# Count and selection behind the first experts, and output products over two blocks, in a convolution, attention and experts kernel

## The chip, the cores and the metric

The kernel runs on one core of a Trainium2 chip. The metric is the device time of one execution in microseconds (us). Everything is computed in 32-bit floating point.

## The reference

The input `x` has the shape (4, 128, 64, 64): four images, 128 channels, 4096 positions each. Two layers follow each other. The first is a convolutional attention: group normalisation, three 1x1 convolutions with PReLU, a softmax over 4096 x 4096 scores for each image, and the result added to `x`. The second works on the 4096 positions as tokens of 128 numbers: a layer normalisation and a causal attention with eight heads and cumulative sums, added to the tokens; then the part that this change is about:

```
logits = einsum('bsd,ed->bse', x, gate_w) + gate_b        # 64 experts
probs = softmax(logits, axis=1)                           # over the 4096 tokens
vals, idx = top_k(probs.transpose(0, 2, 1), 8)            # 8 tokens for each expert
pooled = the 8 gathered tokens, weighted by vals          # one row per image and expert
h = gelu([pooled, 1] @ weight1)                           # 128 -> 512
out = [h, 1] @ weight2                                    # 512 -> 128
outputs.at[idx].add(out * vals)                           # back to the 8 tokens
```

The experts' output is added to the tokens and turned back to channels by positions.

## The kernel before

**Layout.** The tile `t` holds 128 chunks of 128 tokens, that is 32 blocks of 512 tokens, eight for each image. The gate's logits of image `b` are kept in `lg[b]` as 128 partitions (two halves of a block times 64 experts) by 8 x 256 numbers. The first 2,200 us are the attention of layer 0 and the loop over the 32 blocks of layer 1. While the loop runs, the gate's logits, the eight greatest of each block, the candidates' rows (gathered by GpSimd from a table in DRAM) and, for images 0 to 2, the count, the selection and the pooling are spread over it by a plan (`make_plan`, slots named by block and place).

**Order.** TensorE (PE) has the order of the program everywhere. VectorE (DVE), ScalarE (ACT) and GpSimd (POOL) have it for `loop()` and `last_choice()`; for `experts()` and `stores()` the framework's scheduler places their instructions. Each engine works through its own queue in order. SyncE (SP) issues nearly all DMAs, in order too.

**The end of the kernel** is what the change touches.

- `last_choice()` (from L1434) finishes image 3, whose last block is complete only when the loop ends. ACT takes the root of the variances (`gate_root`, L1236), DVE the reciprocals (`gate_close`, L1243), ACT and DVE together normalise (`gate_norm`), PE turns (`gate_turn`, L1275) and multiplies (`gate_logits`, L1282), DVE adds the bias and takes the eight greatest (L1290). They are merged with those of the seven earlier blocks; a product with `swap` (`pw`, L1453) brings the other half's. ACT takes the exponentials (`ce`, `chd`, and L1473 for the whole of `lg`), DVE spreads the candidates' weights (`dd`, L1379), and PE pools the gathered tokens (`pp`, L1486, L1493, L1497). A product gives the sums of the exponentials (`pq`, L1502), their reciprocal is spread over partitions (`dr`, L1505; `pr`, L1510), and `pooled` is written (L1515).
- `fill` (L1419) and `put_back` (L1431) turn blocks of `t` to channels by positions in the meantime: PE transposes four chunks to PSUM, and a copy writes them back. Ten blocks are turned here, the other 22 by `turn_back` (L1583, L1584) under the experts.
- `count` (L1350) counts how many logits reach the eighth greatest, in two pieces of 1,024 columns; `select` (L1358) sets the others to zero in 2,048 columns. For image 3 `late_choice()` calls both. The count serves only a check (`late_count`, `row_check`); the selection is needed by the last stage.
- `experts()` goes over 16 groups of four experts. `first(g)` (L1620) multiplies the pooled rows by `weight1`, `turn(g)` (L1631, L1637, L1642) turns, adds the bias and applies GELU, `second(g)` (L1649) multiplies by `weight2`. An expert's weights are 512 KB. 21 experts find a place before (`load_into`, L1572); the other 43 are loaded in halves, `reload1` (L1558) and `reload2` (L1565), each into the place of an expert whose product is done. Twice `spread` (L1664, L1668) brings the experts' rows to `eo`.
- `z_at` are small selection matrices for `spread`; POOL builds them (L1593, L1595).
- `stores()` (L1703 to L1719) goes over the 32 blocks: two products (one for each half) of `eo` with the selected logits, each of 256 columns, into a PSUM tile of which there are two; DVE adds the tile to `t` (L1714), or in every fifth block ACT copies it (L1711) and POOL adds it (L1712); SP writes two blocks to DRAM at a time, at both ends one.

Of the kernel before, what the change touches and what calls it, by code (L numbers as in the profile page):

```python
# [17 lines left out]
def conv_attn_hybrid_kernel(  # L18
# [809 lines left out]
    def fast():  # L828
# [405 lines left out]
        def gate_root(m, count):  # L1234
# [4 lines left out]
            )  # L1239

        def gate_close(m, count):
            at = slice(ring(m), ring(m) + count)
            nc.vector.reciprocal(env.grs[:, at], env.grs[:, at])  # L1243
            nc.vector.scalar_tensor_tensor(  # L1244
                out=env.gnb[:, at], in0=env.gmv[:, at, :, 0:1].rearrange("p m c o -> p m (c o)"),
                scalar=-1.0, in1=env.grs[:, at], op0=ALU.mult, op1=ALU.mult,
            )
# [98 lines left out]

        def count(b):
            st = sel[b]
            for j in range(2):
                nc.vector.tensor_scalar(  # L1350
                    out=env.e2b[:, :HD], in0=flat_lg(b, CPB * j, CPB * j + CPB),
                    scalar1=st["ce"][:, 16:17], scalar2=None, op0=ALU.is_ge, op1=ALU.add,
                    accum_out=st["sums"][:, 2 + j : 3 + j],
                )
# [78 lines left out]
        def last_choice():  # L1433
# [42 lines left out]
            )  # L1476
            put_back(8, act, 2)
            cw = weigh_candidates(b)
# [16 lines left out]
            for h in range(2):  # L1495
                for j in range(2):
                    nc.tensor.matmul(  # L1497
                        pp, x2[:, 2 * h + j, :], ct[:, j, h * E : (h + 1) * E],
                        start=False, stop=(h == 1 and j == 1),
                    )  # L1500
            pq = ps.tile([P, BLK], F32, tag="t", name="f_pq3")
            nc.tensor.matmul(pq[:, 0:1], env.pair, sums[:, 0:1], start=True, stop=True)  # L1502
# [15 lines left out]

        def late_choice():
            count(B - 1)  # L1520
            select(B - 1)

# [52 lines left out]
        def slot_of(room, i):  # L1575
            return room[:, bass.ts(i, HD)]
# [9 lines left out]
        def experts():  # L1586
# [4 lines left out]
            ]  # L1591
            for b, z in enumerate(z_at):
                nc.gpsimd.memset(z, 0.0)  # L1593
                for h in range(2):
                    nc.gpsimd.tensor_copy(  # L1595
                        z[:, 32 + h * E : 64 + h * E].rearrange("p (g u) -> p g u", u=QG),
                        ident.rearrange("p (u g b) -> p b g u", u=QG, b=B)[:, b],
                    )
            fb1s = env.e1b[:, HD : HD + E * FC].rearrange("p (e c) -> p e c", c=FC)
# [7 lines left out]
            for tile_ in hold:  # L1607
                nc.gpsimd.memset(tile_, 0.0)
            hr = env.rest.tile([P, FH], F32, tag="xl", name="f_hr", bufs=3)

            def own(tile_, g):
# [85 lines left out]
        def stores():  # L1697
            for n in range(NB):
                b, k = blocks[n]
                sc = ps.tile([P, 2, BLK], F32, tag="kv", name=f"f_sct_{n}", bufs=2)  # L1700
                for h in range(2):
                    half = slice(h * E, (h + 1) * E)
                    nc.tensor.matmul(  # L1703
                        sc[:, h, :HB], env.eo[half, b, :], env.lg[b][half, k, :],
                        start=True, stop=True,
                    )
                at = bass.ds(n * CPB, CPB)
                view = t[:, at, :].rearrange("p (h c) x -> p h (c x)", h=2)
                if n % 5 == 3:
                    part = env.rest.tile([P, 2, HB], F32, tag="xl", name=f"f_scs_{n}", bufs=3)  # L1710
                    nc.scalar.copy(part, sc[:, :, :HB])  # L1711
                    nc.gpsimd.tensor_tensor(view, view, part, ALU.add)  # L1712
                else:
                    nc.vector.tensor_add(view, view, sc[:, :, :HB])  # L1714
                ends = n < 2 or n >= NB - 2
                if ends or k % 2:
                    lo = n if ends else n - 1
                    at = bass.ds(lo * CPB, (n + 1 - lo) * CPB)
                    nc.sync.dma_start(  # L1719
                        out=out[b, :, bass.ds((lo % NBLK) * BLK, (n + 1 - lo) * BLK)],  # L1720
                        in_=t[:, at, :].rearrange("p i c -> p (i c)"),
                    )
# [316 lines left out]
        def make_plan():  # L2039
# [55 lines left out]
            at(NB - 1, "T", merge_halves, B - 1)  # L2095
            at(NB - 1, "T", gathers, B - 1, 0, 8)

        def loop():
# [71 lines left out]
            assert not plan, plan.keys()  # L2170

        with tc.manual_schedule(engines={mybir.EngineType.PE}):
            layer0(env)
# [4 lines left out]
            with tc.manual_schedule(  # L2178
# [5 lines left out]
                last_choice()  # L2184
            for room in (slot_of(env.ama, 0), slot_of(env.ama, 1), slot_of(env.ama, 2),
                         slot_of(env.ama, 3), env.wvs,
                         env.held[:, bass.ts(3, HD)]):
                load_into(room)
            for i in range(CPB):
                load_into(slot_of(env.amb, i))  # L2190
            load_into(slot_of(env.e2a, 0))
            load_into(slot_of(env.e2a, 1))
            load_into(slot_of(env.e1b, 0))
            load_into(env.e1b[:, 5 * BLK : 7 * BLK])
            experts()
            stores()
        fp.close()
# [73 lines left out]
```

## Time and profile before

| what | value |
|---|---|
| median of three runs | 2334.75 us (2324.92 to 2334.96) |
| the profiled execution | 2316.78 us, span 2315.1 us |
| PE busy | 2246.9 us (97%) |
| DVE busy | 1439.6 us (62%) |
| ACT busy | 1086.3 us (47%) |
| POOL busy | 196.6 us (8%) |
| mean granted TensorE clock | 0.994 |
| DMA | 105.82 MB, mean 46 GB/s |

The span is the time from the first to the last instruction. PEld is the load of a stationary operand into TensorE, which overlaps with PE. A row of a group names the line of the program, the engine, the operation, output and inputs, shapes and count; then its busy time in us and the mean of one in ns, and the idle time of the engine just before it with what ended most of it. A timeline row begins with start and duration in us. A row of stretches gives for each engine the busy us and the number of instructions, then the clock that TensorE was granted as a share of full speed, the busy share of the DMA engines, and GB/s. A product in 32-bit numbers appears as two matmul instructions, so "x8" is four products.

### The profile page before, as it was taken

How to read it: one execution, taken by the hardware profiler on the slowest of the kernel's cores; microseconds unless marked ns; L12 is line 12 of the kernel's file. 1: busy time of each engine (PE TensorE's matmuls, PEld its weight loads, DVE VectorE, ACT ScalarE, POOL GpSimd, SP SyncE). 2: the span in 40 equal slices, each digit the busy share in tenths (PEclk: the TensorE clock that was granted, in tenths of full speed). 3: DMA queues.
4: the chain of work that ended last, by engine and by line, in shares of the span. 5: the costliest groups of instructions: out<-in, count | busy, mean ns of one | idle time of the engine just before them, and what ended most of it. 6: DMA issues, size and time to landing. Idle time of an engine off the chain costs nothing.

```text
span 2315.1 us, 43294 instructions
## 1 busy us (share of the span) xinstructions
PE 2246.9 (97%) x18418; PEld 1174.0 (51%) x18418; DVE 1439.6 (62%) x2332; ACT 1086.3 (47%) x1324; POOL 196.6 (8%) x365
## 2 busy tenths in 40 slices
PE   7999999999999999999999999999999999999987
PEld 3544444444444444444444444455655656656653
DVE  7666565655665565565556666567777777875623
ACT  2343333433333443334454544445665666665641
POOL 0000000000000000000000000012212222123401
PEclk9999999999999999999999999999999999999989
DMA  2000010000010000001000000011111121114577
GB/s 79 30 12 17 9 45 8 17 8 9 17 45 9 9 17 8 9 12 40 9 5 5 5 10 5 20 44 35 47 58 48 49 64 46 52 57 135 186 261 288
DMA packets 79067, 105.82 MB, mean 46 GB/s; under 512 B 9232, under 2 KB 45072, under 8 KB 78864
## 3 DMA queue, kind: packets, MB, share of 16 engines
q1 hardware_dynamic: 77264, 99.81, 13.7%
q8 instruction: 146, 2.39, 0.4%
q0 software_dynamic: 1024, 2.10, 0.3%
q10 hardware_dynamic: 576, 1.05, 0.1%
q14 instruction: 57, 0.47, 0.1%
HBM read 79.60 MB, written 17.04 MB: 42 GB/s over the span
## 4 chain that ended last, share of the span: by engine, by line
PE 88%; DVE 5%; ACT 3%; DMA 3%; issue 1%; SPq 0%; POOL 0%; ACTq 0%; DVEq 0%; POOLq 0%
PE av L1887 36%; PE sc L1862 18%; PE f_pv L1128 9%; PE f_pk L973 8%; PE f_pt L1151 3%; PE f_po L1174 2%; PE pd L1913 1%; PE f_po L1186 1%; PE pa L1835 1%; PE pe L1809 1%; ACT f_e1a L980 1%; DMA x<-in_x_dram 1%; PE f_pl L1282 1%; PE otr L1925 1%; PE f_ltr L965 1%
## 5 line engine op out<-in xcount | busy, mean ns | idle before, releaser
L1887 PE MATMUL av<-pr,am 64*128 64x512 f32 x4096 | 976.4, 591 | 3.0 <-ACT pr L1867 3.0
L1867 ACT ACTIVATE pr<-sc 128x1024 f32<-128x1024 f32 x512 | 523.6, 1023 | 781.3 <-PE sc L1862 768.1
L1874 DVE TENSOR_TENSOR acc<-acc,pr 128x1024 f32<-128x1024 f32 x480 | 586.5, 1222 | 484.2 <-ACT pr L1867 479.9
L1887 PEld LDWEIGHTS av<-pr,am 64*128 64x128 f32 x4096 | 401.2, 187 | 472.6 <-issue 457.1
L1862 PE MATMUL sc<-e,e 64*128 64x512 f32 x2048 | 534.5, 591 | 4.8 <-DMA e<-side 4.8
L1862 PEld LDWEIGHTS sc<-e,e 64*128 64x128 f32 x2048 | 201.4, 187 | 236.3 <-issue 228.6
L1128 PE MATMUL f_pv<-f_held,f_ama 128*32 128x256 f32 x4096 | 237.5, 381 | 5.7 <-ACT f_e1a L980 4.6
L973 PE MATMUL f_pk<-f_held,f_ama 128*128 128x512 f32 x512 | 234.9, 603 | 0.0
L1133 ACT ACTIVATE f_amb<-f_pv 128x1024 f32<-128x1024 f32 x128 | 130.7, 1023 | 125.2 <-PE f_pv L1128 125.1
L981 DVE TENSOR_TENSOR f_e1a<-f_e1a,f_held 128x1024 f32<-128x1024 f32 x128 | 156.6, 1224 | 48.7 <-ACT f_e1a L980 48.4
L980 ACT ACTIVATE f_e1a<-f_pk 128x1024 f32<-128x1024 f32 x128 | 129.9, 1025 | 119.4 <-PE f_pk L973 54.7
L1128 PEld LDWEIGHTS f_pv<-f_held,f_ama 128*32 128x32 f32 x4096 | 129.5, 110 | 99.7 <-ACT f_e1a L980 10.9
L982 DVE TENSOR_REDUCE f_e1a<-f_e1a 128x8 f32<-128x1024 f32 x128 | 155.3, 1218 | 3.5
L973 PEld LDWEIGHTS f_pk<-f_held,f_ama 128*128 128x128 f32 x512 | 92.5, 190 | 108.6 <-issue 101.0
L1092 POOL COPY f_held<-f_e1a 32x32 f32<-32x32 f32 x128 | 30.8, 240 | 892.8 <-DVE f_e1a L1074 559.1
L918 POOL MEMSET f_held<- 128x1024 f32 x1 | 1.0, 956 | 1036.0 <-DVE xn L1800 1036.0
L1151 PE MATMUL f_pt<-f_amb,f_held 128*32 128x128 f32 x1920 | 83.1, 276 | 0.8 <-ACT f_amb L1133 0.8
L1151 PEld LDWEIGHTS f_pt<-f_amb,f_held 128*32 128x32 f32 x1920 | 59.9, 109 | 10.3 <-issue 5.2
L1192 DVE TENSOR_TENSOR t<-t,f_po 128x512 f32<-128x512 f32 (+1 forms) x33 | 22.1, 671 | 56.7 <-PE f_po L1186 56.7
L956 ACT ACTIVATE f_xl<-t,ln_nb,ln_rs 128x128 f32<-128x128 f32 x128 | 52.8, 490 | 0.9 <-PE pa L1835 0.9
L1263 ACT ACTIVATE f_x<-t,f_gnb,f_grs 128x128 f32<-128x128 f32 x126 | 51.3, 482 | 0.4 <-DVE f_gnb L1244 0.4
L1871 DVE COPY acc<-pr 128x1024 f32<-128x1024 f32 x32 | 22.2, 694 | 39.3 <-ACT pr L1867 39.3
(271 smaller groups left out, 1809.2 us busy)
## 6 DMA issues: line engine op xcount, KB each, us to landing
f_e2a<-f_rd SPq DMA_DIRECT2D x128, 128.0 KB, 3.2
xr<-in_xtok_dram SPq DMA_DIRECT2D x32, 256.0 KB, 2.7
f_table<-f_x SPq DMA_DIRECT2D x62, 128.0 KB, 2.4
out_dram<-t SPq DMA_DIRECT2D x14, 512.0 KB, 3.8
x<-in_x_dram SPq DMA_DIRECT2D x12, 512.0 KB, 5.1
e<-e SPq DMA_DIRECT2D x32, 128.0 KB, 2.2
f_ama<-f_rd SPq DMA_DIRECT2D x16, 256.0 KB, 3.8
f_e1b<-f_rd SPq DMA_DIRECT2D x16, 256.0 KB, 5.1
```

What stands on the lines that cost most here:

```text
L956: nc.scalar.activation(xl[:, c, :], t[:, b * NCH + i, :], AF.Identity, bias=ln_nb[:, b, i : i + 1], scale=ln_rs[:, b, i : i + 1],)
L973: nc.tensor.matmul(pk[:, i, :], xt_at(n)[:, bass.ts(c, P)], env.wks[:, bass.ts(i, BLK)], start=True, stop=True,)
L980: nc.scalar.activation(flat, pk.rearrange("p i x -> p (i x)"), AF.Silu)
L981: nc.vector.tensor_mul(ks, ks, env.qb)
L982: nc.vector.tensor_reduce(s[:, (n % GB) * CPB + c, :], ks, AX.X, ALU.add)
L1128: nc.tensor.matmul(pv[a * CH : (a + 1) * CH, i, :], xt_at(m)[:, bass.ts(c * NA + i, CH)], env.wvs[:, bass.ts(a, HH * C)], start=True, stop ...
L1133: nc.scalar.activation(env.amb[:, bass.ts(c, HD)], pv.rearrange("p i x -> p (i x)"), AF.Silu)
L1151: nc.tensor.matmul(env.pt[i * CH : (i + 1) * CH, :], lhs, rhs, start=i not in env.begun, stop=False, skip_group_check=True,)
L1862: nc.tensor.matmul(sc[:, u, :], e2[halves[u], p, :], e1[halves[u], cols], start=True, stop=True,)
L1867: nc.scalar.activation(pr, sc, AF.Exp)
L1874: nc.vector.tensor_add(acc, acc, pr)
L1887: nc.tensor.matmul(av, am[h, j, :], pr[h, u, :], start=(j == 0), stop=(j == NCH - 1))
```

## The change

The diff does five things.

1. ACT, DVE and POOL keep the order of the program through `load_rooms()` (the former loop of loads, now a function), `experts()` and `stores()`.
2. `late_choice(g)` puts the two pieces of image 3's count behind the additions of groups 0 and 1, and the selection behind that of group 2. The check on the counts moves from group 2 to group 3, and POOL builds the selection matrices at group 2 instead of ahead of the experts.
3. `root_table()`, a square root of one column, is planned at the last block's slot "T", behind the last SiLU, so that ACT loads the table of the root there.
4. `last_choice()` turns twelve blocks instead of ten; the copies are distributed anew between ACT and DVE, and the exponential of the whole `lg` comes ahead of two of them. The experts turn 20 blocks.
5. `stores()` goes over 16 pairs of blocks. Each product covers 512 columns. DVE adds both blocks of a pair in one instruction of 1,024 columns; in every third pair ACT copies the first block, POOL adds it and DVE adds the second; the first and the last pair are added in two pieces. The number of writes and their sizes stay.

In the order of the instructions, SP's is unchanged. On DVE the two reductions of `rows` and the four products with `den` (`fb2r`) stand behind group 3's addition instead of earlier. In a mixed pair, DVE's addition waits for ACT's copy of the same tile.

```diff
+        def root_table():
+            nc.scalar.activation(env.gnb[:, 0, 0:1], eps5, AF.Sqrt)
...
-        def count(b):
+        def count(b, lo=0, hi=2):
             st = sel[b]
-            for j in range(2):
+            for j in range(lo, hi):
...
-            for n, tag in enumerate(("kv", "kv", "kv", "kv", "t", "o")):
+            for n, tag in enumerate(("kv", "kv", "kv", "kv", "t", "o", "kv", "kv")):
                 fill(n, tag, n % 2)
             put_back(0, act, 2)
             gate_root(m, 1)
...
             put_back(2, act, 2)
             gate_turn(m, dve)
-            fill(6, "kv")
+            fill(8, "kv")
             gate_logits(m)
-            put_back(4, dve)
-            fill(7, "kv", 1)
+            put_back(6, act, 2)
+            fill(9, "kv", 1)
...
-            fill(8, "kv")
-            fill(9, "kv", 1)
+            fill(10, "kv")
+            fill(11, "kv", 1)
...
-            put_back(5, act)
-            put_back(6, act, 2)
...
-            put_back(8, act, 2)
+            put_back(4, act)
+            put_back(10, act, 2)
...
+            put_back(8, dve, 2)
             pp = sm("f_pp3", E)
...
+            put_back(5, dve)
             pq = ps.tile([P, BLK], F32, tag="t", name="f_pq3")
...
-        def late_choice():
-            count(B - 1)
-            select(B - 1)
+        def late_choice(g):
+            if g < 2:
+                count(B - 1, g, g + 1)
+            elif g == 2:
+                select(B - 1)
...
             first(0)
-            n = 10
+            n = 12
             for g in range(EG):
                 turn(g)
-                if g == 0:
-                    late_choice()
-                for _ in range(2 if g < NB - 10 - EG else 1):
+                late_choice(g)
+                for _ in range(2 if g < NB - 12 - EG else 1):
                     turn_back(n)
                     n += 1
                 if g + 1 < EG:
                     first(g + 1)
                 if g == 2:
+                    selections()
+                if g == 3:
                     late_count()
                     row_check()
...
-            for n in range(NB):
+            for n in range(0, NB, 2):
                 b, k = blocks[n]
                 sc = ps.tile([P, 2, BLK], F32, tag="kv", name=f"f_sct_{n}", bufs=2)
                 for h in range(2):
                     half = slice(h * E, (h + 1) * E)
                     nc.tensor.matmul(
-                        sc[:, h, :HB], env.eo[half, b, :], env.lg[b][half, k, :],
+                        sc[:, h, :], env.eo[half, b, :],
+                        env.lg[b][half, k : k + 2, :].rearrange("p k x -> p (k x)"),
                         start=True, stop=True,
                     )
...
-                if n % 5 == 3:
+                ends = n == 0 or n == NB - 2
+                if n // 2 % 3 == 1:
                     part = env.rest.tile([P, 2, HB], F32, tag="xl", name=f"f_scs_{n}", bufs=3)
-                    nc.scalar.copy(part, sc[:, :, :HB])
-                    nc.gpsimd.tensor_tensor(view, view, part, ALU.add)
+                    nc.scalar.copy(part, scv[:, 0])
+                    nc.gpsimd.tensor_tensor(view[:, 0], view[:, 0], part, ALU.add)
+                    nc.vector.tensor_add(view[:, 1], view[:, 1], scv[:, 1])
+                elif ends:
+                    for i in range(2):
+                        nc.vector.tensor_add(view[:, i], view[:, i], scv[:, i])
                 else:
-                    nc.vector.tensor_add(view, view, sc[:, :, :HB])
+                    nc.vector.tensor_add(view, view, scv)
...
             at(NB - 1, "T", gathers, B - 1, 0, 8)
+            at(NB - 1, "T", root_table)
...
                 loop()
                 last_choice()
-            for room in (slot_of(env.ama, 0), slot_of(env.ama, 1), slot_of(env.ama, 2),
...
-            experts()
-            stores()
+                load_rooms()
+                experts()
+                stores()
```

More of the change, by code (lines that the diff above doesn't have):

```diff
@@ L1591, in experts @@
             ]
[L1592 to L1598, printed above, removed]
             fb1s = env.e1b[:, HD : HD + E * FC].rearrange("p (e c) -> p e c", c=FC)
@@ L1609, in experts, with selections @@
             hr = env.rest.tile([P, FH], F32, tag="xl", name="f_hr", bufs=3)
+            def selections():
+                for b, z in enumerate(z_at):
+                    nc.gpsimd.memset(z, 0.0)
+                    for h in range(2):
+                        nc.gpsimd.tensor_copy(
+                            z[:, 32 + h * E : 64 + h * E].rearrange("p (g u) -> p g u", u=QG),
+                            ident.rearrange("p (u g b) -> p b g u", u=QG, b=B)[:, b],
+                        )
             def own(tile_, g):
@@ L1703, in stores @@
                     nc.tensor.matmul(
-                        sc[:, h, :HB], env.eo[half, b, :], env.lg[b][half, k, :],
+                        sc[:, h, :], env.eo[half, b, :],
+                        env.lg[b][half, k : k + 2, :].rearrange("p k x -> p (k x)"),
                         start=True, stop=True,
                     )
-                at = bass.ds(n * CPB, CPB)
-                view = t[:, at, :].rearrange("p (h c) x -> p h (c x)", h=2)
-                if n % 5 == 3:
-                    part = env.rest.tile([P, 2, HB], F32, tag="xl", name=f"f_scs_{n}", bufs=3)
-                    nc.scalar.copy(part, sc[:, :, :HB])
-                    nc.gpsimd.tensor_tensor(view, view, part, ALU.add)
-                else:
[L1714 to L1718, printed above, removed]
+                scv = sc.rearrange("p h (k x) -> p k h x", k=2)
+                at = bass.ds(n * CPB, 2 * CPB)
+                view = t[:, at, :].rearrange("p (k h c) x -> p k h (c x)", k=2, h=2)
+                ends = n == 0 or n == NB - 2
+                if n // 2 % 3 == 1:
+                    part = env.rest.tile([P, 2, HB], F32, tag="xl", name=f"f_scs_{n}", bufs=3)
+                    nc.scalar.copy(part, scv[:, 0])
[4 more added lines that the diff above has]
+                        nc.vector.tensor_add(view[:, i], view[:, i], scv[:, i])
+                else:
+                    nc.vector.tensor_add(view, view, scv)
+                step = 1 if ends else 2
+                for i in range(0, 2, step):
                     nc.sync.dma_start(
-                        out=out[b, :, bass.ds((lo % NBLK) * BLK, (n + 1 - lo) * BLK)],
-                        in_=t[:, at, :].rearrange("p i c -> p (i c)"),
+                        out=out[b, :, bass.ds((k + i) * BLK, step * BLK)],
+                        in_=t[:, bass.ds((n + i) * CPB, step * CPB), :].rearrange("p i c -> p (i c)"),
                     )
@@ L2170, in loop, with load_rooms @@
             assert not plan, plan.keys()
+        def load_rooms():
+            for room in (slot_of(env.ama, 0), slot_of(env.ama, 1), slot_of(env.ama, 2),
+                         slot_of(env.ama, 3), env.wvs,
+                         env.held[:, bass.ts(3, HD)]):
+                load_into(room)
+            for i in range(CPB):
+                load_into(slot_of(env.amb, i))
+            load_into(slot_of(env.e2a, 0))
+            load_into(slot_of(env.e2a, 1))
+            load_into(slot_of(env.e1b, 0))
+            load_into(env.e1b[:, 5 * BLK : 7 * BLK])
         with tc.manual_schedule(engines={mybir.EngineType.PE}):
@@ L2184, in fast @@
                 last_choice()
-            for room in (slot_of(env.ama, 0), slot_of(env.ama, 1), slot_of(env.ama, 2),
[L2186 to L2194, printed above, removed]
-            experts()
-            stores()
+                load_rooms()
+                experts()
+                stores()
         fp.close()
```

## The prediction, made before the changed kernel ran

> **What bounds the kernel now.** I read four views, in this order: the stretches of the last 130 us (which engine, which clock, how much DMA), the chain of waits there, DVE's timeline around the choice, and the groups of the last stage. The change touches only what comes after about 2183 us of a span of 2315.1 us, so nothing before that counts.
>
> The stretches are cut on a grid of 3.41 us, because the granted clock falls at 2196.38 and rises at 2220.26, seven such steps apart. Columns: busy us of PE, PEld, DVE, ACT, POOL, then the granted clock, the DMA share and GB/s.
>
> ```profile
> 2189.55:2192.97 3.42, 3.02 (x36) 2.60 (x24) 2.22 (x10) 2.09 (x2) 2.51 (x4) 1.00 0.96 346
> 2192.97:2196.38 3.41, 1.56 (x12) 1.04 (x12) 1.63 (x5) 2.94 (x6) 2.50 (x4) 1.00 1.03 400
> 2196.38:2199.79 3.41, 3.32 (x16) 2.45 (x13) 2.32 (x9) 0.93 (x3) 3.10 (x9) 0.50 0.60 202
> ...
> 2203.21:2206.62 3.41, 3.39 (x17) 3.30 (x16) 0.45 (x2) 1.26 (x3) 0.00 (x0) 0.50 0.24 65
> 2206.62:2210.03 3.41, 0.66 (x2) 0.50 (x2) 3.41 (x7) 0.00 (x0) 0.00 (x0) 0.50 0.22 89
> 2210.03:2213.45 3.42, 1.44 (x8) 0.20 (x8) 1.92 (x4) 0.00 (x0) 2.23 (x6) 0.50 0.00 0
> ...
> 2216.86:2220.27 3.41, 3.41 (x35) 1.69 (x37) 0.00 (x0) 1.62 (x3) 0.00 (x0) 0.50 0.45 144
> 2220.27:2223.69 3.42, 3.42 (x60) 2.46 (x56) 0.23 (x1) 1.48 (x4) 0.15 (x1) 1.00 0.77 265
> ```
>
> PE stands idle for half of 2192.97 to 2196.38 and then runs at half clock for 24 us. DVE alone works from 2206.6 to 2212. DMA is nearly unused from 2200 to 2214.
>
> ```profile
> 2214.00:2228.00 14.00, 12.18 (x126) 8.17 (x126) 1.60 (x8) 7.51 (x14) 0.30 (x2) 0.78 0.70 235
> 2228.00:2277.00 49.00, 45.01 (x604) 27.56 (x604) 4.30 (x19) 17.41 (x39) 1.82 (x12) 1.00 1.05 385
> 2277.00:2284.00 7.00, 5.67 (x82) 4.28 (x82) 2.14 (x7) 0.73 (x2) 0.00 (x0) 1.00 0.20 74
> 2284.00:2308.00 24.00, 20.17 (x120) 9.03 (x120) 16.85 (x26) 3.51 (x6) 7.62 (x6) 1.00 0.79 311
> ```
>
> The experts are bound by their weights: 49 us at a full DMA share. 21 of 64 experts have a place before the first product; 43 x 0.524 MB = 22.5 MB follow and take 58.5 us at 385 GB/s. The first reload is issued at 2213.95, when the first product has released its weights, and the last lands at 2277.1. So **the end of this stage is the first reload plus 58.5 us plus the DMA's idle time**, and what comes before the first reload counts in full. DVE's timeline shows what delays it:
>
> ```profile
> 2206.39 1.28 DVE L1350 TENSOR_SCALAR_CACHE_REDUCE f_e2b<-f_lg,f_ce 128x1024 f32<-128x1024 f32 x1 [2.96 <-PE f_pp L1497]
> ...
> 2207.71 1.28 DVE L1350 TENSOR_SCALAR_CACHE_REDUCE f_e2b<-f_lg,f_ce 128x1024 f32<-128x1024 f32 x1
> ...
> 2209.08 2.35 DVE L1358 SCALAR_TENSOR_TENSOR f_lg<-f_lg,f_ce 128x2048 f32<-128x2048 f32 x1
> ...
> 2211.70 0.26 DVE L1515 TENSOR_TENSOR f_pooled<-f_pp,f_e1b 128x64 f32<-128x64 f32 x1
> ```
>
> The count (twice) and the selection stand between the sums and `pooled`, which the first expert product needs at 2212.01. In the last stage, the groups:
>
> ```profile
> L1703 PE MATMUL f_sct<-f_lg,f_e1b 64*128 64x256 f32 x128 | 21.3, 426 | 3.4 <-DVE t L1714 1.9 <-DVE f_e1b L1668 0.4
> L1714 DVE TENSOR_TENSOR t<-t,f_sct 128x512 f32<-128x512 f32 x26 | 17.3, 686 | 7.0 <-PE f_sct L1703 3.8 <-ACT f_scs L1711 2.6
> ```
>
> Neither engine is full: two PSUM tiles go round, and one round is 0.73 (products) + 0.70 (addition) + 0.08 us for two blocks; with ACT's blocks 25.05 us for 32.
>
> **The change, part by part.**
>
> *Root's table.* ACT loads it at 2191.89 for 1.28 us, and the root runs at 2193.19; its input is ready at 2192.25. In the new order load and a 128x1 root stand behind the last SiLU, in an idle of 7.83 us. Gain 2192.30 against 2193.19: 0.89 us (between 0, if statistics were later, and 1.30). The Trainium skill (ScalarE: Activation LUTs, "What ACT_TABLE_LOAD costs") gives 1.28 us of load plus 1.38 us of drain, 2.66 in all; by it the gain might be 2.7. The row decides: root follows the load after 0.02 us, and the statistics limit it.
>
> *Fills moved.* Blocks 6 and 7 are turned before the last gate's transposes: 8 x 0.11 = 0.88 us, 2192.3 to 2193.4, ended before x comes at 2193.6. Block 8's fill now waits for ACT's second copy and stands ahead of the logits on PE: about 0.15 us lost. DVE's copy of block 4 (0.59) leaves the chain, but behind it the merge also waited for `pw`, which came at 2198.66: I count 0. DVE's new copy of 1024 columns (two of 512 at 0.67, so 1.2) lies beside `pp` and ends within 0.3 us of when `ct` can start; PE has four products to do meanwhile: 0. If that cover fails it costs up to 1.2. Of 22 turns back under the experts 20 remain (0.87 us of PE fewer, hidden by DMA: 0).
>
> *The clock.* This is the largest unknown. PE's gaps with the new order are, by the rows: 0.13 before the gate's transposes, 0.46 before block 8, 0.6 before `pw`, 1.08 before `pp`, then 0.55 and 0.5 around `pr`, 0.64 before the first turn. No 3.41 us then has less than about 1.7 us of busy PE. In the trace windows with 1.56 and 1.34 us lost the clock; windows with 1.67 and 1.78 kept it. Against this stands the Trainium skill (TensorE: Matmul & The Clock Gate, "Part 4: PE-mode transpose"): transposes do not count as busy in the same way. By it four more fills protect nothing, and the clock falls as before. The first row above speaks the other way: 2189.55 to 2192.97 held nearly only transposes, and the clock stayed at 1.00. But 2203.21 to 2206.62, busy 3.39 us with narrow products, did not bring it back. I take the row: clock kept, not safely. If kept: logits 0.22 and `pw` 0.20 faster, with the waits between 0.55; `pp` and its neighbours, 6.0 us at half clock, take 24 x 0.125 (16 took 2.00 earlier) + 0.6 = 3.6, so 2.4 less; the first product 1.0 less.
>
> *Count and selection behind the experts.* 2206.60 (sums' product ended) to 2212.01 is 5.41 us. Left are reciprocal 0.19, spread 0.25, product `pr` 0.35 (0.66 at half clock), copy 0.25, multiplication 0.3: 1.4 us (1.7). Gain 4.0 (3.7). The moved 1.28, 1.28 and 2.35 us queue on DVE after the additions of groups 0, 1, 2; behind each waits the next group's addition, 3.36 us later at full clock, so they are covered. If that cover fails, the selection delays a group by at most 2.3. The row check goes to group 3 with two more short reductions (about 0.5 us of PE waiting, by then under the DMA). POOL's selections (some 2 us) move off `pr`'s and `pooled`'s region to before group 3's clearing, which has a group's time: 0. The DMAs stand in the same order on SP: the 86 reloads come earlier by what PE gains.
>
> *Sum to the first reload, clock kept:* 0.89 - 0.15 + 0.55 = 1.3; + 2.4 + 4.0 + 1.0 = 8.7 us. And DMA's idle time of 14 x 0.30 = 4.2 us between 2214 and 2228, of which some 1.2 is the first landing, came from PE at half clock; at full clock some 2.8 go. The weights end 11.5 us earlier.
>
> *Two blocks per product.* The trace has no 64x512 product of this kind here; L1862's have 591 ns, and L1887's follow each other at 976.4/4096 = 0.24: 3 x 0.24 + 0.59 = 1.30 us for a pair. The addition of 1024 columns: 1.22 (L1874's row, both operands in SBUF) to 1.37 (two of 686); I take 1.22. A round is 1.30 + 1.22 + 0.08 for two pairs, 1.30 a pair against 1.57. In the five mixed pairs DVE waits for ACT's copy of the same tile: 1.30 + 0.62 + 0.69, the same round. 16 x 1.30 + 1.4 = 22.2 against 25.05: 2.8. But writing 8.39 MB at 390 GB/s takes 21.5 us: first issue at 2.05 after the first product (1.5 now), about 2.0 to data, 21.5, 0.5 lost: 26.1 against 28.15 now. **The writes become the bound**; I take 2.0 (between 0 and 2.8).
>
> Total 11.5 + 2.0 = 13.5 us. The profiled execution took 2316.78 us, 18 below the median of 2334.75; I subtract from the median and allow for that scatter: 2321.
>
> **The rivals.** *A, clock kept throughout:* 2321, 0.58. *B, the clock falls in the gaps around the first product:* 1.3 + 2.4 + 3.9 + 2.0 = 9.6, so 2325; for it, the gaps leave only 1.7 us; 0.18. *C, the clock falls as before:* 0.7 + 3.7 + 2.0 = 6.4, so 2328; for it the skill's rule, and that the narrow products count little; 0.19. *D, slower:* the clock falls, and count and selection on DVE leave a gap in each of the first groups, so that no window is full and it does not rise. At half clock a group takes 6.7 us of PE against 5.4 of DMA; 16 groups would end at 2315 instead of 2277, up to 2370. It decides from about seven groups at half clock. Against it: from group 4 on the order is as before, and there the clock was 1.00. 0.05. In A or C the pairs may also bring nothing (2323, 2330).
>
> **How the numbers follow.** 0.5% is 11.7 us, about what a measurement of this kernel can tell from no change. A lies 2 us beyond it, and the runs before lie 10 us apart: 0.46 of 0.58 faster, the rest same. B gives 0.05 and 0.13, C 0.03 and 0.16, D 0.04 slower and 0.01 same. Sum: faster 0.54, same 0.42, slower 0.04. The range takes in A with runs as low as the profiled one, B and C: 2308 to 2332.
>
> **What would show it.** Right: clock 1.00 from 2190 on, first expert product near 2204, first reload near 2205, weights landed near 2266, full DMA share within 8 us of the first reload, 16 pairs in about 22 us with the write share near 1. Wrong: a row at 0.50 after 2196; DVE's additions waiting behind L1353 or L1361; a pair above 1.57 us.

## The result, and the profile after

| | median of 8 runs each | lowest to highest |
|---|---|---|
| before | 2332.48 us | 2324.92 to 2338.03 |
| after | 2320.09 us | 2317.06 to 2321.46 |

The ratio is 0.9949 (95% interval 0.9934 to 0.9965): 12 us faster, between 8 and 15. The forecast was 2321 from 2334.75, a gain of 13.5.

The two profiled executions can't be laid side by side by their spans. That of before took 2316.78 us, below all eight of its runs here; that of after 2321.39 us, near the top of its own. In some sets of runs every profile has a delay of some 9 us at the last gate, and before takes about 2332 us (2325 to 2339), in others no profile has it, and before takes about 2320 (2316 to 2325), so each ratio below is against before on the same chip in the same set. The profile on which the prediction rests is one without the delay; that of after has it. VectorE's timeline of after, start, duration, engine, line, operation, and in brackets the idle time before it and what the profile holds to have ended it:

```profile
2194.90 0.14 DVE L1320 TENSOR_SCALAR f_neg<-f_top 128x1 f32<-128x1 f32 x1
2203.73 0.75 DVE L1192 TENSOR_TENSOR t<-t,f_po 128x256 f32<-128x256 f32 x2 [8.69 <-remote]
...
2218.92 0.17 DVE L1507 RECIPROCAL f_den<-f_pq 128x1 f32<-128x1 f32 x1 [0.77 <-PE f_pq L1506]
...
2220.22 0.27 DVE L1519 TENSOR_TENSOR f_pooled<-f_pp,f_e1b 128x64 f32<-128x64 f32 x1
2223.61 0.22 DVE L1645 TENSOR_TENSOR f_hs<-f_htr,f_e1b 128x64 f32<-128x64 f32 x1 [3.11 <-PE f_htr L1639]
2223.75 1.27 DVE L1353 TENSOR_SCALAR_CACHE_REDUCE f_e2b<-f_lg,f_ce 128x1024 f32<-128x1024 f32 x1
...
2227.84 0.23 DVE L1645 TENSOR_TENSOR f_hs<-f_htr,f_e1b 128x64 f32<-128x64 f32 x1 [2.82 <-POOL f_e1b L1612]
2227.98 1.27 DVE L1353 TENSOR_SCALAR_CACHE_REDUCE f_e2b<-f_lg,f_ce 128x1024 f32<-128x1024 f32 x1
...
2231.15 0.22 DVE L1645 TENSOR_TENSOR f_hs<-f_htr,f_e1b 128x64 f32<-128x64 f32 x1 [1.89 <-PE f_htr L1639]
2231.29 2.34 DVE L1361 SCALAR_TENSOR_TENSOR f_lg<-f_lg,f_ce 128x2048 f32<-128x2048 f32 x1
```

The last addition into the tokens waits 8.69 us (1.09 in the profile shown of before), and "remote" names nobody: the product that it needs had ended. What the change was for is below it: between the reciprocal and `pooled` stand 1.3 us where count and selection stood before, and these now follow the additions of groups 0, 1 and 2; the next addition always comes after they have ended.

ScalarE's timeline shows root's table where the change puts it, and the same delay, on the first copy of turned blocks. Of its 15.71 us some 8 are the delay; that copy waited 7.83 in the profile shown of before:

```profile
2189.47 1.28 ACT L1242 ACT_TABLE_LOAD   x1
...
2206.67 1.01 ACT L1434 COPY t<-f_etb 128x1024 f32<-128x1024 f32 x1 [15.71 <-remote]
2207.58 0.30 ACT L1236 ACTIVATE f_grs<-f_gmv,eps 128x4 f32<-128x4 f32 x1
```

The stretches of after, cut at the steps of its clock (columns as in the prediction):

```profile
2195.00:2203.00 8.00, 4.03 (x60) 2.93 (x50) 0.04 (x1) 0.00 (x0) 6.12 (x7) 0.90 0.91 336
2203.00:2211.60 8.60, 4.95 (x22) 4.25 (x24) 3.85 (x15) 4.47 (x7) 2.45 (x4) 0.50 0.26 89
2211.60:2221.90 10.30, 7.30 (x56) 5.21 (x54) 6.05 (x19) 5.04 (x8) 0.00 (x0) 1.00 0.17 52
2221.90:2225.30 3.40, 2.90 (x16) 2.58 (x20) 1.42 (x3) 2.61 (x5) 0.00 (x0) 0.50 0.71 223
2225.30:2237.00 11.70, 11.36 (x166) 7.41 (x162) 4.40 (x8) 6.48 (x14) 2.80 (x15) 1.00 0.85 291
```

VectorE and ScalarE do nothing for 8 us while GpSimd's gathers run; the clock falls behind that, comes back for the choice, and falls once more 1.3 us behind the start of the first expert product (2220.55). The last stage, groups and then four of its stretches:

```profile
L1712 PE MATMUL f_sct<-f_lg,f_e1b 64*128 64x512 f32 x64 | 17.5, 635 | 2.9 <-DVE t L1730 1.0 <-DVE t L1725 0.8 <-DVE t L1728 0.6
L1730 DVE TENSOR_TENSOR t<-t,f_sct 128x1024 f32<-128x1024 f32 x9 | 10.9, 1220 | 0.6 <-PE f_sct L1712 0.4
```

```profile
2292.00:2296.00 4.00, 2.93 (x14) 0.93 (x12) 3.38 (x5) 0.59 (x1) 1.27 (x1) 1.00 0.47 179
2296.00:2300.00 4.00, 3.67 (x16) 0.90 (x12) 3.13 (x4) 0.59 (x1) 1.27 (x1) 1.00 0.94 376
2300.00:2304.00 4.00, 3.61 (x16) 0.90 (x12) 3.33 (x4) 0.59 (x1) 1.27 (x1) 1.00 1.02 400
2304.00:2308.00 4.00, 3.65 (x14) 0.90 (x12) 3.31 (x4) 0.59 (x1) 1.27 (x1) 1.00 1.02 408
```

The share reaches 1.02 and stays: the writes bound this stage now.

### The profile page after: what moved, and what is told of

Its sections match the earlier page's. It is cut to its first block, busy times and chain, and to the rows that moved or that the text cites. A ratio compares the mean times of both kernels' runs of the same rounds, so it can differ in the third digit from the quotient of the medians.

```text
span 2319.7 us, 43135 instructions
## 1 busy us (share of the span) xinstructions
PE 2247.9 (97%) x18354; PEld 1171.3 (50%) x18354; DVE 1440.9 (62%) x2325; ACT 1085.9 (47%) x1322; POOL 193.5 (8%) x364
## 3 DMA queue, kind: packets, MB, share of 16 engines
q0 software_dynamic: 1024, 2.10, 0.4%
## 4 chain that ended last, share of the span: by engine, by line
PE 88%; DVE 4%; ACT 3%; DMA 3%; issue 1%; another core or an unknown queue 1%; SPq 0%; POOL 0%; ACTq 0%; DVEq 0%; POOLq 0%
PE av L1901 37%; PE sc L1876 19%; PE f_pv L1128 9%; PE f_pk L973 8%; PE f_pt L1151 3%; PE f_po L1174 2%; PE pd L1927 1%; PE pa L1849 1%; PE pe L1823 1%; PE f_po L1186 1%; ACT f_e1a L980 1%; PE f_pl L1285 1%; DMA x<-in_x_dram 1%; PE otr L1939 1%
## 5 line engine op out<-in xcount | busy, mean ns | idle before, releaser
L1881 ACT ACTIVATE pr<-sc 128x1024 f32<-128x1024 f32 x512 | 524.2, 1024 | 783.4 <-PE sc L1876 773.5
L1133 ACT ACTIVATE f_amb<-f_pv 128x1024 f32<-128x1024 f32 x128 | 130.8, 1024 | 126.3 <-PE f_pv L1128 124.2
```

The lines of the kernel that those rows point to most:

```text
L1133: nc.scalar.activation(env.amb[:, bass.ts(c, HD)], pv.rearrange("p i x -> p (i x)"), AF.Silu)
L1881: nc.scalar.activation(pr, sc, AF.Exp)
```

## The experiments

**Which part brings what.** In e1, `stores()` of the changed kernel stands in the kernel before; in e2 the reverse.

> The kernel before with only the output stage changed: products and additions over two blocks. By the prediction's sum the writes become the bound and the kernel is 2.0 us faster than before (0 to 2.8). If the pairs bring nothing (their rival), the time is that of before within 0.5 us. The two traces, read from the first store product to the last DMA, say more than either: 28.15 us in before and some 26.1 in after, so that a gain of about 2 us is expected from them; but in after the writes start while the DMA has just finished the weights, and a part of the 2 us may depend on that. In its profile the stores' product should stand at 16 pairs in about 22 us with the DMA share near 1.

Measured: ratio 0.9988 (0.9979 to 0.9997), 2.8 us faster than before (0.7 to 4.9). From the first product to the last byte written e1 takes 26.5 us; both profiles of before take 29.6, after 26.4. The pairs do bring something, 3.1 us by the traces.

> The changed kernel with the output stage of before (one block per product). By the prediction's sum it keeps 11.5 of the gain and loses the 2.0 of the pairs: about 10.4 us faster than before with the measured total of 12.4. If the pairs bring nothing, 12.4 us faster, as the changed kernel; if the pairs are most of the gain (7 us or more), under 5 us faster. Its profile also tells whether the idle time of VectorE (8.7 us) and ScalarE (15.7 us) at the last gate, which the profile of the changed kernel shows and that of before doesn't, comes again: if it belongs to the new order, it should be there at its full length.

Measured: 0.9969 (0.9958 to 0.9980), 7.2 us faster than before. Less than the 10.4 expected: without the pairs 4.7 us of the gain are gone by the ratios, 3.4 by the traces (29.8 us from the first product of the stores to the last byte). The difference lies within the intervals. VectorE's idle time was there again, 7.13 us.

In e3 count and selection go back; their calls behind `turn(g)` go:

```
             nc.tensor.matmul(pq[:, 0:1], env.pair, sums[:, 0:1], start=True, stop=True)
+            late_choice(0)
             nc.vector.reciprocal(env.den[:, b : b + 1], pq[:, 0:1])
+            late_choice(1)
...
+            late_choice(2)
             pr = ps.tile([P, BLK], F32, tag="x", name="f_pr3")
```

> The changed kernel with the count (twice) and the selection put back on VectorE between the sums' product and pooled, where before has them. The prediction prices their move at 4.0 us (5.41 less 1.4); in the two traces the way from the sums' product to the first expert product is 5.41 and 1.65 us, so 3.8. Theory: 3.8 to 4.0 us slower than the changed kernel, as the first reload comes that much later and the weights are the bound. Rival: the DMA's idle time behind the first reload takes up the difference (the weights' queue has other work, or the clock decides), and it is less than 1 us slower. Second rival: the gap also costs the clock, and it is 6 us slower or more.

Measured: 0.9972 (0.9963 to 0.9982), 6.5 us faster than before, so some 5.5 slower than after by the two ratios. After ran in other sets, and the intervals of the two ratios leave some 4 us to either side of such a difference, here and below. VectorE's timeline of e3:

```profile
2217.38 1.28 DVE L1353 TENSOR_SCALAR_CACHE_REDUCE f_e2b<-f_lg,f_ce 128x1024 f32<-128x1024 f32 x1 [0.68 <-PE f_pp L1500]
...
2218.58 0.16 DVE L1508 RECIPROCAL f_den<-f_pq 128x1 f32<-128x1 f32 x1
2218.70 1.28 DVE L1353 TENSOR_SCALAR_CACHE_REDUCE f_e2b<-f_lg,f_ce 128x1024 f32<-128x1024 f32 x1
...
2220.07 2.35 DVE L1361 SCALAR_TENSOR_TENSOR f_lg<-f_lg,f_ce 128x2048 f32<-128x2048 f32 x1
...
2222.58 0.27 DVE L1522 TENSOR_TENSOR f_pooled<-f_pp,f_e1b 128x64 f32<-128x64 f32 x1
```

Here 4.0 us lie between the reciprocal and `pooled`, and the count's first piece stands ahead of both. From the end of the sums' product to the first expert product it is 5.5 us, against 1.7 in after, the 3.8 expected. Its clock was also halved for 10.2 us around the first experts, against 3.4 in after and 6.8 in a second profile of it, a2. Whether that costs the rest, and so which of the theory and the second rival holds, the times can't tell.

In e4 `last_choice()` is that of before (ten fills in their old places), the rest as changed.

> The changed kernel with the ten fills of before in their old places (turns back of ten blocks in the last choice, 22 under the experts) and the rest as changed: root's table ahead, count and selection behind the first experts, pairs. The prediction gives the fills the clock: 0.55 + 2.4 + 1.0 us, and 1.2 to 2.8 us of DMA idle time behind them; so by the theory it is 4 to 6.5 us slower than the changed kernel, and its profile shows a granted clock of 0.50 from the last gate to the first experts. If the clock doesn't hang on the fills (rival C's reason, or the throttle's own grid decides from one execution to the next), it is within 1 us of the changed kernel.

Measured: 0.9969 (0.9957 to 0.9981), 7.2 us faster than before, some 5 slower than after. Its stretches:

```profile
2211.31:2214.73 3.42, 2.36 (x20) 2.03 (x20) 2.67 (x12) 2.03 (x5) 0.00 (x0) 1.00 0.02 5
2214.73:2228.38 13.65, 11.61 (x60) 7.97 (x63) 2.76 (x8) 6.25 (x9) 0.00 (x0) 0.50 0.36 115
```

The clock that after keeps through `pp` up to the first expert product is gone here for 13.65 us. That agrees with the theory in one execution; its rival, the place of the clock's steps, is not out (more on it in the next section).

**The delay.** If it belongs to the change, it ate part of the gain; if not, it is in before too.

> The kernel before, unchanged, for a second profile. In the profile shown of it, the addition into the tokens at the last gate starts on VectorE at 2189.89 us and nothing waits; in the five profiles of the changed kernel and its variants, one of which has the order of before up to the output stage, it starts at 2198.8 to 2203.7 us, 7 to 8.7 us after the product that it needs, because TensorE's semaphore counts reach the other engines late while GpSimd issues the last eight gathers. Theory: the kernel before has this delay too in most executions, and the shown profile (2316.78 us, when its other runs take 2325 to 2338) is one without it; the addition then starts near 2199 and the time is near 2330. Rival: the delay belongs to the changed kernel and to what was compiled with it; then the addition starts near 2190 and the time is near 2317.

Measured: 2334.86 us, and on VectorE of this second profile of before:

```profile
2195.43 0.14 DVE L1317 TENSOR_SCALAR f_neg<-f_top 128x1 f32<-128x1 f32 x1
2204.26 0.75 DVE L1192 TENSOR_TENSOR t<-t,f_po 128x256 f32<-128x256 f32 x2 [8.68 <-remote]
```

8.68 us, as long as in after. The theory stands: the delay is not the change's.

> The changed kernel, unchanged, beside the kernels that follow on one chip. 12 us faster than before (10 to 14), and in its profile the late counts of TensorE at the last gate again (7 to 9 us on VectorE, some 15.5 on ScalarE). If the delay comes and goes from one execution to the next, its profile may be without it; then the first expert product comes near 2210 instead of 2220.5.

Measured: 0.9947 (0.9934 to 0.9960), 12.4 us faster, with 8.63 us of idle time on VectorE and 15.62 on ScalarE. The semaphore events of the trace say what is late. In after, the count of a product that started at 2194.90 us landed at 2195.22; those of products that started at 2195.34, 2195.77 and 2197.14 landed at 2197.93, 2203.71 and 2206.65. The second of these lets VectorE go (2203.73), the third ScalarE (2206.67). GpSimd meanwhile:

```profile
2195.05 0.94 POOL L1334 DMA_INDIRECT f_e1b<-f_table,f_at  x1 [12.28 <-DVE f_neg L1320]
2196.30 0.95 POOL L1334 DMA_INDIRECT f_e1b<-f_table,f_at  x1 [0.30 <-issue]
...
2203.80 0.95 POOL L1334 DMA_INDIRECT f_e1b<-f_table,f_at  x1 [0.30 <-remote]
```

In g1 the last eight gathers are left out: `at(NB - 1, "T", gathers, B - 1, 0, 8)` goes.

> The changed kernel without the last eight gathers (the rows of the last batch's candidates are left out; the product runs on rows that lay there before). Theory: TensorE's counts are late because GpSimd's gathers hold them up: in all five profiles the last late count came 1.7 to 1.9 us after the end of the eighth gather. Without them VectorE's addition follows its product within 1.2 us, ScalarE's first copy within 1 us of its fills, and the first expert product comes some 9 to 10 us earlier; the kernel is 8 to 12 us faster than the changed one. Rival 1: the weights that stream in at 350 to 390 GB/s in the same stretch hold the counts up; then the delay stays (7 us or more on VectorE) and the time changes by less than 2 us. Rival 2: the delay goes, but the weights bound what follows and less than 4 us are gained.

Measured: 0.9923 (0.9909 to 0.9937), 18.0 us faster than before and 6.3 faster than the changed kernel (a2) in the same set (medians 2314.41 and 2320.67). VectorE's timeline of g1, first at the gathers of image 2, which stay:

```profile
2172.63 0.48 DVE L1289 TENSOR_SCALAR f_lg<-f_pl,f_gbs 128x256 f32<-128x256 f32 x1 [2.90 <-remote]
...
2197.85 0.14 DVE L1320 TENSOR_SCALAR f_neg<-f_top 128x1 f32<-128x1 f32 x1
2199.07 0.75 DVE L1192 TENSOR_TENSOR t<-t,f_po 128x256 f32<-128x256 f32 x2 [1.07 <-PE f_po L1186]
```

The delay is gone, with the weights streaming at 402 GB/s (2199 to 2203 us): the gathers are needed for it. It is not that this execution was one without the delay, for at image 2's gathers it was held up by 2.90 us, as in a2 (2.80), and the executions without the delay have no such wait. The first expert product comes 15.7 us behind the last maximum instead of 25.3 in a2, as expected. The gain in time is smaller than the 8 to 12 expected. In this execution five isolated steps of half clock (17 us in all) had made it 7 us later than a2, which had none, by the time of the last maximum; whether its other runs were as late, the times alone do not tell.

In g2 six of the eight gathers wait until the merged maximum is known; `places` computes their row numbers, which before are ready with the others:

```
             nc.vector.tensor_copy(both[:, 16:17], top[:, 7:8])
+            places(b, 2, 8)
+            gathers(b, 2, 8)
```

> The changed kernel with six of the last eight gathers behind the choice of the last block (their places are computed behind the merged maximum on VectorE; two stay where they were). If the gathers hold up TensorE's counts, the last gate's chain runs without the delay, and the six gathers (6 x 1.25 = 7.5 us, and some 2 us to land) then stand before the products that read them: first expert product 1 to 4 us earlier than in the changed kernel, and 0 to 4 us faster. If the weights hold the counts up, the delay stays and the gathers come on top: 5 to 8 us slower than the changed kernel.

Measured: 0.9960 (0.9948 to 0.9973), 9.3 us faster than before, so about 3 slower than after. The addition waited only 3.06 us behind two gathers, but the six late ones held `pp` back: it took 11.4 us to the end of the sums' product, against 3.5. Half clock, 23.89 us of it, had begun 4.2 us before the first late gather (2204.86), so they did not start it:

```profile
2200.64:2224.53 23.89, 18.04 (x72) 12.45 (x76) 7.70 (x23) 8.87 (x13) 6.73 (x8) 0.50 0.27 75
```

The first expert product came 26.5 us behind the last maximum, against 25.4 in after and a2: neither forecast. The delay shrinks with the gathers in front, but their time has to go somewhere.

> The kernel before without the last eight gathers (the rows of the last batch's candidates are left out), as the counterpart of the changed kernel without them (0.9923 of before, 18 us less). It tells what the change brings where TensorE's counts are not held up. By the traces the hold-up costs the kernel before 9.6 us up to root and about 11.3 us to the end. Theory: this kernel is 10 to 12 us faster than before (ratio 0.9949 to 0.9957), so that the change brings 6 to 8 us without the gathers by the times, or 12 by the stages of the traces. Rival: part of the hold-up is hidden in the kernel before (its chain waits elsewhere), and it gains less than 7 us. If before runs near 2320 us in this call, the hold-up is absent from it, and this kernel gains less than 2 us.

Measured: 1.0002 (0.9993 to 1.0011), with before at 2321.40: the last clause of the expectation. Where the delay is absent the gathers cost nothing. What g0 would do where the delay is present is not known.

**Root's table and the weights.** In r1 `at(NB - 1, "T", root_table)` goes.

> The changed kernel without root's table loaded ahead (the one-element root behind the last SiLU is left out). The prediction prices it at 0.89 us. In the traces with TensorE's late counts the load of 1.28 us stands behind ScalarE's late copy, where nothing else hides it: from the last maximum to root 13.8 and 13.9 us without and 12.3 to 12.5 us with the load ahead, 1.4 apart. Theory: 0.9 to 1.4 us slower than the changed kernel, so 10.6 to 11.5 us faster than before. Rival: ScalarE's slack takes it up and the time is that of the changed kernel within 0.3 us.

Measured: 0.9971 (0.9961 to 0.9980), 6.7 us faster than before, not 10.6 to 11.5, with before at 2319.66 and no delay. Its root comes 4.39 us behind the maximum; in v1, the next kernel, of the same set, 3.46. That is the prediction's 0.89 us. But r1's first reload comes 22.25 us behind the maximum and v1's 16.79, 5.5 us apart: with this longer gap the clock fell at 2198.66 for 20.5 us, and in v1 not at all. In these two executions a gap of 0.9 us went with a loss of six times its length. The times agree (medians 7.0 us apart, every run of v1 below every run of r1), but v1 has a second edit, and r1's steps fall elsewhere, so that the gap alone did it is not shown.

In v1 the second group's products move up, in v2 all groups' by one:

```
             first(0)
+            product(1)
...
-                if g + 1 < EG:
+                if g == 0:
+                    copied(1)
+                elif g + 1 < EG:
                     first(g + 1)
```

> The changed kernel with the second group's expert products directly behind the first group's, before its transposes. It tests why the weights need some 65 us behind the first reload instead of the 58.5 at full rate: in every trace, at half and at full clock, only 2.5 to 2.9 MB land in the first 12 us, where 4.6 could. Theory: the chain of the first group (copy, transposes, addition, GELU) frees the weights too late, the clock matters little; with the second group's first halves (1.05 MB, 2.7 us at 385 GB/s) freed some 3 us earlier the weights end 1.5 to 2.7 us sooner, and the kernel is 1.5 to 2.7 us faster than the changed one. Rival: the clock is what limits (the prediction's step), so that nothing is gained (within 0.5 us), or the products' second wait costs as much as it gains.

Measured: 0.9942 (0.9928 to 0.9956), 13.5 us faster than before. The 12 us behind the first reload and the rest up to the last weights, of g1 and of v1:

```profile
2214.78:2226.78 12.00, 11.23 (x156) 8.23 (x156) 5.32 (x8) 7.38 (x14) 2.62 (x14) 0.86 0.77 244
2226.78:2279.09 52.31, 46.68 (x610) 28.03 (x600) 6.53 (x31) 16.71 (x39) 1.81 (x12) 1.00 1.03 377
```

```profile
2210.81:2222.81 12.00, 11.60 (x172) 8.16 (x164) 5.55 (x9) 7.75 (x16) 2.78 (x15) 1.00 0.88 291
2222.81:2274.90 52.09, 46.08 (x595) 27.16 (x594) 6.30 (x29) 16.64 (x38) 1.67 (x11) 1.00 1.01 368
```

The DMA fills up sooner, 291 instead of 244 GB/s. But v1 also has full clock there, and g1 0.86 of it; no trace with the old order has full clock through these 12 us, so whether order or clock did it is open. Then v1 moves 368 instead of 377, and the weights end 64.1 instead of 64.3 us behind the first reload: against g1 nothing is left of it.

> As the kernel with the second group's products early, but with every group's products two groups ahead of its transposes. If the weights bound all 16 groups, this gains the same 1.5 to 2.7 us at the start and up to 1 us at the end, where the last weights to land are second halves and less work stands behind them: 2 to 3.5 us faster than the changed kernel. Rival: the products wait for weights that land later in the queue and hold up the second products behind them on TensorE; then it is slower than the kernel with only the second group early.

Measured: 0.9951 (0.9938 to 0.9965), 11.4 us faster than before; weights 62.75 us behind the first reload. Neither v1 nor v2 ran in one set with after, after never ran in a set without the delay, and the intervals overlap with its 0.9949 and 0.9947: that one of them is better is not shown.

## Why the prediction was right, point by point

Stages of the traces, each from its own start, in us. "With the delay": mean of b2 and e1 (before's order up to the stores) against mean of after and a2. "Without": mean of the profile shown of before and g0, against g1.

| stage | predicted gain | with the delay | without |
|---|---|---|---|
| last maximum to root | 0.89 | 13.86 to 12.50: 1.4 | 4.39 to 3.47: 0.9 |
| root to `pp` | 0.40 | 7.75 to 7.77: 0.0 | 7.44 to 7.10: 0.3 |
| `pp` to end of sums' product | 2.4 | 5.61 to 3.46: 2.1 | 6.03 and 3.43 to 3.47: 2.6 or 0 |
| to first expert product | 4.0 | 5.41 to 1.67: 3.7 | 5.39 to 1.67: 3.7 |
| to first reload | 1.0 | 1.95 to 1.33: 0.6 | 1.95 to 1.08: 0.9 |
| to last weights landed | 2.8 | 66.57 to 66.69: -0.1 | 65.79 to 64.31: 1.5 |
| first product of the stores to last byte | 2.0 | 29.59 to 26.32: 3.3 | 29.60 to 26.39: 3.2 |

- **Root's table.** 0.9 without the delay. With it 1.4, since the load then stands behind the late copy with nothing beside it. The 2.66 us of load plus drain that the Trainium skill gives (ScalarE: Activation LUTs, "What ACT_TABLE_LOAD costs") were rightly set aside: in before root follows the load after 0.02.
- **Count and selection.** Confirmed, 3.7 for 4.0, and in their new places the next addition never waits for them: rival D is out.
- **The clock.** Right in the choice, wrong as "kept throughout": after lost it behind the delay (10.2 us) and around the first expert product (3.4 us, in a2 6.8), which is rival B's place. Without the delay, v1 had none of it there, g1 and v2 one step, and r1 20.5 us. The mark by which the prediction judged, that 1.67 us of busy PE in a step keep the clock, doesn't hold: steps with 1.90 (after, 2218.45), 2.20 (g0) and 2.62 us (v2) lost it. Nor do busy us alone decide. The first of e4's rows above and the first row here, of after, both hold 2.36 us of busy PE. Behind that of e4, with fewer turned blocks, the clock was lost; behind that of after it was kept. The second row here, of a2, holds transposes and nothing else, and full clock came back behind it:

```profile
2211.62:2215.03 3.41, 2.36 (x18) 1.51 (x16) 2.02 (x10) 1.40 (x3) 0.00 (x0) 1.00 0.02 5
2203.15:2206.57 3.42, 2.87 (x14) 2.87 (x15) 0.95 (x5) 2.98 (x6) 0.00 (x0) 0.50 0.00 0
```

  In before 3.39 us of narrow products (2203.21) had not brought it back. So these traces speak against the Trainium skill's rule that transposes don't count as busy in the same way (TensorE: Matmul & The Clock Gate, "Part 4: PE-mode transpose"), by which the fills would be worth nothing. But g0, with the ten fills of before, kept full clock through `pp`, and r1, with twelve, did not: where the steps of 3.41 us fall decides too, and what a step needs is open.
- **The failed step: DMA's idle time, -2.8 us.** The prediction charged 4.2 us of it to half clock and the first landing, and let 2.8 go at full clock; the runs give 1.5 without the delay and -0.1 with it. In the 12 us behind the first reload the share is 0.69 (208 GB/s) in b2, 0.73 (235 and 236) in after and a2, and 0.77 in g1; in after it was full only from 12 us on, not within 8. From b2 to after that is 27 x 12 / 385 = 0.8 us. In a2 the rest ran at 355 GB/s instead of 371, and the 0.8 was gone. Two things were wrong. The clock wasn't full there: after, a2 and g1 had 3.4 to 5.7 us of half clock in these 12 us. And the rate behind them was set at 385; it was 371 in after and 368 in v1. In v1, at full clock, the share was full from 8 us on, but with the second group's products moved up; even there the stage took 64.1 us, a gain of 1.7. How much of the idle time is the clock and how much the first group's chain is open. The base was misread too: in before the last weights landed at 2279.2, not 2277.1.
- **The stores, 3.3 instead of 2.0.** After was forecast at 26.1 and takes 26.3, with the writes as the bound: right. Before was set at 28.15, but it is 29.6 up to the last byte: the mis-sized term is the old stage. A pair's products took 4 x 0.27 = 1.09 us, not 1.30; the addition 1.22 as said.
- **The base.** The sum came from an execution without the delay and was subtracted from a median with it. The 18 us between them were taken for scatter; some 12 are the delay. That the sum held all the same is luck: the delay is as long in both kernels (8.68 and 8.69 us), which the prediction could not know.

With the delay the stages sum up to 11.0 us (11.8 without), the medians say 12.4. The number came nearer than its parts: the weights gave 2.9 less than forecast and the stores 1.3 more. Of the marks for "right", those up to the first reload are met only without the delay: first expert product forecast 15.2 us behind the last maximum (2204), in g1 15.7; first reload 16.2, in g1 16.8; last weights 77, in g1 81, which is the failed step. Full clock all the way only v1 had.

The parts don't add up one by one. Undone alone, the pairs cost 5 us, the count's move 5.5, the fills 5, more than the 12 of all, but each is uncertain by some 4 us. In the traces of e3 and e4 half clock lasts longer than in after, which may be what their costs share. The order of the program on VectorE, ScalarE and GpSimd, which the change also keeps, was not undone alone.

## What to carry to other kernels

When a profiled execution is far below the median of its runs, look for a wait that the others may have before building on it, and compare traces by stages from a common event, not by spans. Near a throttled clock, price a gap by the half clock that it may start, not by its length. Before crediting a queue with the idle time at its start, see what its rate becomes afterwards.

## What the runs showed of the hardware that was not expected

- While GpSimd issues gathers back to back (eight, each 0.94 us and 0.30 apart), TensorE's semaphore counts can land up to 9.8 us after their products started (a2; 0.3 otherwise). In after, b2, e1, e2, e3, e4 and a2 the last late count came 1.7 to 1.9 us after the eighth gather had ended, and the same executions, g1 and g2 too, have a hold-up of 2.1 to 2.9 us at the gathers of image 2, some 30 us earlier. In the profile shown of before, in r1, v1 and v2 the same gathers held up nothing. Within each set that was profiled more than once, all profiles had it or none; kernels without it in one set ran on the same chip as kernels with it in another. What decides is open, and so is the mechanism. The weights alone do not do it (g1); that they take part beside the gathers was not tried; the hold-up of image 2 came at 99 to 178 GB/s, not at 390.
- The granted clock moves in steps of 3.41 us, and single steps of half clock fall elsewhere too: at some 23, 70, 1170, 1485 and 2137 us in one execution or another, 0 to 17 us in sum ahead of the last maximum. In the changed kernel that maximum came at 2191.1 us in the execution with none (a2) and at 2195.0 in the one with four: such steps may be a good part of the scatter between runs.
